# Mean squares by quarters of tokens in column tiles, PSUM banks kept whole in a planned four-layer graph network

## The chip, the cores and the metric

The kernel runs on one core of a Trainium2 chip. The metric is the device time of one execution in microseconds, lower is better. The time before is the median of three runs. TensorE is called PE in profile rows, its weight loads PEld, VectorE DVE, ScalarE ACT, GpSimd POOL, SyncE SP.

## The reference

There are 64 graphs of 256 nodes with 256 features, and each has a dense 256x256 matrix `adj` of edge weights. Four layers follow each other; each is `x = layernorm(x + f(x, adj))`, all in float32.

```python
# layer 0: sigmoid attention of 4 heads, scaled by degrees
att = sigmoid(q @ k.T / 8) * adj;  deg = att.sum(-1);  A = deg**-.5 * att * deg**-.5;  f = layernorm(A @ v)
# layer 1: softmax attention of 8 heads, masked where adj <= 0
f = softmax(where(adj > 0, q @ k.T / sqrt(32), NEG)) @ v @ Wo + bo
# layer 2: sum over neighbours, then a network of 1024 hidden features
h = (eps * x + adj @ x) @ W1 + b1
f = silu(h * rsqrt(mean(h**2, -1) + 1e-6) * rms_weight) @ W2 + b2
# layer 3: additive attention of one head, layernorm, gelu
f = gelu(layernorm(softmax(where(adj > 0, leaky(s1[:, None] + s2[None, :]), NEG)) @ Wh) * gamma + beta)
```

The change is in layer 2's `mean(h**2, -1)`, the mean over 1024 hidden features for each of the 256 nodes, and in the way in which the order of all instructions is planned.

## The kernel before, in words

A graph's nodes lie in two blocks of 128 partitions (`NB = 2`), its features likewise. `graph()` does not issue instructions. It records operations with `op(engine, cost, fn, writes, reads, ...)`; an `Op` holds a closure `fn` that will issue one or several instructions on one engine, a planned cost in ns, and what it writes and reads (`Value`s, some in parts, such as the two halves of a PSUM tile). All 64 graphs are recorded first.

`Plan.order()` then puts all operations of all graphs into one order. It steps through a model of the five engines, and takes at each step the operation that can start first; among equals, the one that is due first. "Due" comes from turns: every graph has four turns, one for each table of ScalarE (sigmoid, exp, silu, gelu), and layers of different graphs share rounds (`ROUND = 0, 2, 5, 7`: layer 1 of a graph runs two rounds after its layer 0, layer 2 five rounds after, layer 3 seven rounds after). An operation without predecessors (a load) is admitted once its due time lies at most `AHEAD` turns away. Buffers are slots of a kind: `SLOTS` has 42 of "s" (512 words in SBUF), 3 of "b" (2048 words, `hT`), 8 of "p" (the eight PSUM banks), and so on. An operation that takes a buffer has to wait for a free slot.

The model knows modes of TensorE. "full" is a matmul on the whole 128x128 array, "transpose" is a transpose, "rows" has 32 or 64 rows (scores L444 and L524), "columns" has 32 or 64 columns (degrees L462, products with values L484 and L560). `CHANGE` holds the planned costs of going from one mode to another, and `STAY` makes the planner reluctant to leave rows or columns.

`emit()` issues the closures in the planned order. From there every engine works through its own queue in that order; semaphores are set automatically where one instruction depends on another. That tracking goes by whole PSUM banks: a matmul into one half of a bank is ordered against a read of the other half. The plan before counts the halves as independent.

The lines that matter: in layer 2, L591 forms `aggT` (neighbour sums), L603 multiplies it with W1, each PSUM bank taking two blocks of 128 hidden features (i = 0, 1). ScalarE reads each half twice: L608 squares into `sq`, L610 scales into `hT`. L615 adds the squares of the four banks, L617 the two halves. L622 sums over the partitions on TensorE: for each block of 128 nodes, `sq` is the stationary operand and a column `mean_of` of 1/1024 is the moving one, so the mean of a node comes out on its partition. L625 adds the epsilon, L626 (GpSimd) takes the power -1/2, and L631 transposes the two columns, broadcast over 128 columns, into `pr`, a row for each node on all partitions. L635 multiplies `hT` by it, L637 applies silu, L645 multiplies with W2.

In layer 1, L524 makes the scores of four heads at a time (`hq` = 0 and 1), four PSUM banks each, from `qT1` and `kT1` (L510, L311). L407 masks them and finds the row minimum on VectorE, L412 takes exp, L545 transposes on VectorE, L547 and L549 reorder through DRAM, L560 multiplies with `v1`. L565 to L573 bring the reciprocal row sums `r` to the partitions; L567 is a small transpose on TensorE. In layer 0, L462 sums over partitions with a 128x32 operand of ones in four column tiles, and L466 transposes 32x32 blocks of the result on VectorE. L287 is the same kind of transpose on other tiles; L320 and L331 are shared helpers for projections; L275 is the helper for transposes on TensorE; L660 and L669 belong to layer 3.

Of the kernel before, what the change touches and what calls it, by code (L numbers as in the profile page):

```python
# [9 lines left out]
F32 = mybir.dt.float32  # L10
AF = mybir.ActivationFunctionType
OP = mybir.AluOpType

P = 128
# [5 lines left out]
PE_MM, PE_TR = 432, 109  # L20
# [7 lines left out]
DMA_KB, DMA_SEEN = 4, 1900  # L28

WORDS = {"s": 516, "d": 1024, "b": 2048, "c": 32, "p": 512, "h": 1024}  # L30
AHEAD = 14
STAY = 200
NEAR = 1, 1, 3

ROUND = 0, 2, 5, 7
TAIL = 0, 2, 3, 4
# [42 lines left out]
class Plan:  # L79
# [6 lines left out]
        self.ops, self.turns = [], {}  # L86
        self.graph = 0

    def op(self, engine, cost, fn, w=(), r=(), turn=None, mode="full", after=None, size=0):
        pair = lambda x: x if isinstance(x, tuple) else (x, None)  # L90
        w, r = [pair(x) for x in w], [pair(x) for x in r]
        op = Op(engine, cost, fn, w, r, self.graph, turn, mode, after, size)
        op.table = turn is not None and engine == "ACT"
        if op.table:
            self.turns[turn] = self.turns.get(turn, 0) + 1
        self.ops.append(op)

    def order(self):
        for i, op in enumerate(self.ops):
            op.index = i  # L100
        for op in reversed(self.ops):
            op.due = min((nxt.due for nxt in op.after), default=4 * (min(op.graph + ROUND[3], self.graphs - 1 + TAIL[3]) + 1))
            if op.turn is not None:
                op.due = min(op.due, op.turn)
        clock = {e: 0.0 for e in AFTER}
        self.free = {k: [(0.0, i) for i in range(n)] for k, n in SLOTS.items()}
        turns, left = sorted(self.turns), dict(self.turns)
        turn, loaded, mode, moved = 0, None, "full", 0.0
        ready = {op for op in self.ops if not op.waits}
        done = []  # L110
        self.busy = {e: 0.0 for e in AFTER}
        while ready:
            best = None
            for op in ready:
                if (op.due - AHEAD if op.first else op.turn or 0) > turns[turn]:
                    continue
                start = clock[op.engine]
                if op.engine == "PE" and mode in ("rows", "columns") and mode != op.mode:
                    start += STAY - 60 * (op.mode == "transpose")
                start = max(start, op.ready)  # L120
                need = {}
                for v in op.values:
                    if v.slot is None:
                        need[v.kind] = need.get(v.kind, 0) + 1
                for kind, n in need.items():
                    free = self.free[kind]
                    if len(free) < n:
                        break
                    start = max(start, sorted(free)[n - 1][0])
                else:  # L130
                    key = start, op.due, op.graph, op.index
                    if best is None or key < best[0]:
                        best = key, start, op
            if best is None:
                raise RuntimeError(f"the plan is stuck at {len(done)} of {len(self.ops)}")
            _, start, op = best
            op.start = start
            ready.discard(op)
            if op.table and op.turn != loaded:
                op.start, loaded = op.start + TABLE_LOAD, op.turn  # L140
            if op.engine == "PE":
                op.start = max(op.start, clock["PE"] + CHANGE.get((mode, op.mode), 0))
                mode = op.mode
            end = clock[op.engine] = op.start + op.cost
            op.landed = end + op.seen
            if op.engine == "SP":
                moved = max(moved, end) + op.size * DMA_KB
                op.landed = max(op.landed, moved + DMA_SEEN)
            self.busy[op.engine] += op.cost
            done.append(op)  # L150
            op.takes = [v for v in op.values if v.slot is None]
            for v in op.takes:
                self.free[v.kind].sort()
                v.slot = self.free[v.kind].pop(0)[1]
            for v in op.values:
                v.uses -= 1
                v.end = max(v.end, op.landed)
                if not v.uses:
# [12 lines left out]
        return sorted(done, key=lambda op: op.start)  # L171
# [78 lines left out]
def graph(plan, nc, c, t, out, b):  # L250

    op = plan.op
# [264 lines left out]
    for hq in range(H1 // 4):  # L517
        pss = [Value("p", "ps", 2) for _ in range(4)]

        def fn(hq=hq, pss=pss):  # L520
            for n in range(NB):
                for i in range(4):
                    s = slice(i * HD1, (i + 1) * HD1)
                    pe.matmul(two(pss[i])[:, n, :], two(qT1)[s, hq, n * P:(n + 1) * P], two(kT1)[s, hq, :],  # L524
                              start=True, stop=True)
        op("PE", 2 * PE_MM, fn, pss, [qT1, kT1], turn=turn(1, EXP), mode="rows")
        for pair in range(2):
            e = Value("d", "e", 4)
            for i in range(2):
                softmax(pss[2 * pair + i], negmask, HD1 ** -0.5, e,  # L530
                        lambda n, i=i, e=e: e.t[:, 256 * (2 * i + n):256 * (2 * i + n + 1)],
                        lambda n, i=i: 2 * i + n, r, lambda n, h=4 * hq + 2 * pair + i: 2 * h + n, turn(1, EXP))
            if b < NEAR[1]:
                eT = Value("d", "eT", 2)
                for i in range(2):
                    half = lambda v, i=i: v.t[:, 512 * i:512 * (i + 1)].rearrange("p (n c) -> p n c", n=2)
                    ps = Value("p", "ps", 2)
                    transpose(lambda ps=ps: two(ps), lambda e=e, half=half: half(e), ps, e)
                    op("ACT", 466, lambda ps=ps, eT=eT, half=half: act.copy(half(eT), two(ps)), [(eT, i)], [ps])
                eTs.append((eT, lambda i, m, eT=eT: eT.t.rearrange("p (h m c) -> p h m c", h=2, m=2)[:, i, m]))  # L540
                continue


            eb, far, eT = Value("d", "eb"), Value("h", "far"), Value("d", "eT", 4)
            op("DVE", 1155, lambda e=e, eb=eb: dve.transpose(eb.t.rearrange("p (b g i) -> p g b i", b=4, i=32),  # L545
                                                             e.t.rearrange("p (g b i) -> p g b i", b=4, i=32)), [eb], [e])
            op("SP", 420, lambda eb=eb, far=far: nc.sync.dma_start(far.t, eb.t), [far], [eb], after=3500, size=512)  # L547
            for q in range(4):
                op("SP", 420, lambda far=far, eT=eT, q=q: nc.sync.dma_start(  # L549
                    eT.t[32 * q:32 * q + 32].rearrange("j (a g) -> j a g", a=4),  # L550
                    far.t.rearrange("(a j) (b g) -> b j a g", a=4, b=4)[q]), [(eT, q)], [far], after=4000, size=128)
            eTs.append((eT, lambda i, m, eT=eT: eT.t.rearrange("p (a h n k i) -> p h k n a i", a=4, h=2, n=2, k=2)[:, i, m]))
# [65 lines left out]
    ps = Value("p", "ps")  # L618

    def fn(ps=ps, sq=sq):  # L620
        for n in range(NB):
            pe.matmul(ps.t[:, n:n + 1], sq.t[:, n * P:(n + 1) * P], c.mean_of, start=True, stop=True)  # L622
    op("PE", 363, fn, [ps], [sq])
    rs = Value("c", "rs")
    op("DVE", 50, lambda ps=ps: dve.tensor_scalar(rs.t[:, :NB], ps.t[:, :NB], 1e-6, None, op0=OP.add), [rs], [ps])  # L625
    op("POOL", 700, lambda: pool.tensor_tensor(rs.t[:, :NB], rs.t[:, :NB], c.mhalf[:, :NB], OP.pow), [rs], [rs])  # L626
    pr = Value("p", "pr")

# [62 lines left out]
def gnn_stack_kernel(ctx: ExitStack, tc: tile.TileContext, t: dict, out: bass.AP):  # L691
# [25 lines left out]
    make_identity(nc, ident)  # L717
    ones = const.tile([P, 32], F32, name="ones")
    nc.vector.memset(ones, 1.0)
    mean_of = const.tile([P, 1], F32, name="mean_of")  # L720
    nc.vector.memset(mean_of, 1.0 / HID)
    mhalf = const.tile([P, 8], F32, name="mhalf")
    nc.vector.memset(mhalf, -0.5)
# [50 lines left out]
```

## Time and profile before

| | |
|---|---|
| median of three runs | 2768.54 us (2766.03 to 2769.21) |
| profiled execution, its own time | 2761.13 us |
| its span, first to last instruction | 2759.3 us |
| mean granted TensorE clock | 0.996 |
| first matmul starts / last matmul starts | 6.1 us / 2742.4 us |
| L622, TensorE rows of 128x1 | 256 rows, 34.8 us busy |
| L625, DVE | 64 instructions, 147 ns each |
| L626, POOL | 64 instructions, 755 ns each |

Times below are counted from the start of the span. A row of the timeline has start, length, engine, line, operation, tiles, shape and the number of instructions merged in it; a float32 matmul is two instructions there, a transpose one. In the table of stretches, each row has the stretch, its length, busy time and (instruction count) of PE, PEld, DVE, ACT and POOL, then the granted clock, the share of the DMA engines and GB/s. A matmul's length overlaps with the next, so distances between starts are more exact than lengths.

### The profile page before, as it was taken

To read this page: it belongs to the slowest core of one execution; us is meant where nothing else is said; L and a number is where in the kernel's file an instruction comes from. 1 tells how busy PE (TensorE), PEld (TensorE's weight loads), DVE (VectorE), ACT (ScalarE), POOL (GpSimd) and SP (SyncE) were. 2 spreads that over 40 slices of the span, in tenths; PEclk is the share of its full clock that TensorE was granted. 3 is DMA by queue.
4 is the path that set the end of the run, shared out by engine and by line. 5 is a ranking of instruction groups with operands and counts; after the bars stand their busy time and mean duration, and the time that the engine had idled before them with its cause. 6 is when DMAs were issued, how large, how long until landed. Compare 5 with 4: busy or idle time off the path is not lost.

```text
span 2759.3 us, 56034 instructions
## 1 busy us (share of the span) xinstructions
PE 2703.5 (98%) x17280; PEld 2160.5 (78%) x17280; DVE 2443.0 (89%) x7426; ACT 2224.2 (81%) x5323; POOL 574.6 (21%) x902
## 2 busy tenths in 40 slices
PE   8999999999999999999999999999999999999997
PEld 6778777777777777787877877788778777777776
DVE  6989998898898889989989989889989899899966
ACT  4878888778788888788878887888888887888775
POOL 1112222122121121221221212212212122122212
PEclk9999999999999999999999999999999999999999
DMA  5677677676677566766756756757667677576651
GB/s 157 199 210 198 172 204 201 176 205 167 193 215 191 157 192 173 211 176 189 210 161 190 217 158 195 211 152 209 184 176 212 166 189 218 143 206 188 184 135 35
DMA packets 710923, 505.17 MB, mean 183 GB/s; under 512 B 310112, under 2 KB 669920, under 8 KB 710624
## 3 DMA queue, kind: packets, MB, share of 16 engines
q1 hardware_dynamic: 710624, 501.59, 65.9%
q8 instruction: 138, 2.26, 0.3%
q14 instruction: 161, 1.32, 0.2%
HBM read 303.44 MB, written 197.92 MB: 182 GB/s over the span
## 4 chain that ended last, share of the span: by engine, by line
PE 75%; DVE 10%; ACT 6%; DMA 4%; SPq 2%; issue 2%; POOL 0%; DVEq 0%; POOLq 0%; ACTq 0%
PE ps L331 13%; PE ps L320 13%; PE ps L645 13%; PE ps L603 11%; PE ps L444 4%; PE ps L524 4%; PE ps L484 3%; PE av L560 3%; PE ps L660 3%; PE ps L591 3%; ACT e L412 2%; DVE e L407 2%; DVE st L345 1%; DMA eT<-far 1%; PE ps L275 1%
## 5 line engine op out<-in xcount | busy, mean ns | idle before, releaser
L412 ACT ACTIVATE e<-e,low 128x256 f32<-128x256 f32 x1152 | 579.8, 505 | 87.5 <-DVE low L407 86.6
L645 PE MATMUL ps<-w,hT 128*128 128x256 f32 x2048 | 478.8, 383 | 5.5 <-ACT hT L637 4.8
L603 PE MATMUL ps<-aggT,w 128*128 128x256 f32 x2048 | 476.4, 382 | 3.8 <-DVE low L407 1.9
L357 POOL TENSOR_SCALAR mv<-mv 128x2 f32<-128x2 f32 x384 | 123.0, 320 | 1573.3 <-DVE mv L347 1012.1
L645 PEld LDWEIGHTS ps<-w,hT 128*128 128x128 f32 x2048 | 382.4, 191 | 68.1 <-issue 6.7
L603 PEld LDWEIGHTS ps<-aggT,w 128*128 128x128 f32 x2048 | 379.7, 190 | 69.4 <-DVE low L407 11.7
L407 DVE CUSTOM_DVE_ANT_0 e<-ps,adj 128x256 f32<-128x256 f32 x1024 | 361.1, 420 | 12.7 <-PE ps L524 11.2
L545 DVE STREAM_TRANSPOSE eb<-e 128x1024 f32<-128x1024 f32 x252 | 306.2, 1224 | 9.3 <-ACT e L412 9.2
L608 ACT ACTIVATE sq<-ps,b 128x256 f32<-128x256 f32 x512 | 242.0, 480 | 82.7 <-PE ps L603 73.0
L358 POOL TENSOR_TENSOR mv<-mv,mhalf 128x2 f32<-128x2 f32 x384 | 298.6, 778 | 32.0
L610 ACT ACTIVATE hT<-ps,br,r 128x256 f32<-128x256 f32 x512 | 288.8, 575 | 10.2 <-PE ps L645 6.7
L372 ACT ACTIVATE x<-y,mv 128x256 f32<-128x256 f32 x384 | 217.3, 602 | 50.9 <-DVE mv L368 48.9
L345 DVE BATCH_NORM_STATS2 st<-y 128x6 f32<-128x256 f32 x640 | 245.2, 413 | 0.9
L412 ACT ACTIVATION_READ_ACCUMULATOR e<-e,low 128x1 f32 x1152 | 225.4, 196 | 0.0
L615 DVE TENSOR_TENSOR sq<-sq 128x512 f32<-128x512 f32 x192 | 131.0, 682 | 98.1 <-ACT sq L608 97.2
L450 DVE TENSOR_TENSOR att<-att,adjT 128x512 f32<-128x512 f32 x256 | 166.6, 681 | 5.1 <-ACT att L448 5.1
L524 PE MATMUL ps<-kT,qT 32*128 32x256 f32 x2048 | 152.0, 400 | 4.3 <-ACT kT L311 4.2
L635 DVE TENSOR_TENSOR hT<-hT,pr 128x1024 f32<-128x1024 f32 x128 | 149.7, 1209 | 5.3 <-PE pr L631 5.3
L470 POOL TENSOR_TENSOR dp<-dp,mhalf 128x8 f32<-128x8 f32 x64 | 106.8, 1668 | 196.3 <-DVE dp L469 166.2
L448 ACT ACTIVATE att<-ps 128x512 f32<-128x512 f32 x256 | 132.2, 603 | 5.6 <-PE ps L444 3.0
L637 ACT ACTIVATE hT<-hT 128x1024 f32<-128x1024 f32 x128 | 128.9, 1050 | 9.1 <-DVE hT L635 7.9
L524 PEld LDWEIGHTS ps<-kT,qT 32*128 32x128 f32 x2048 | 97.9, 184 | 47.5 <-issue 23.3
(113 smaller groups left out, 5486.0 us busy)
## 6 DMA issues: line engine op xcount, KB each, us to landing
far<-eb SPq DMA_DIRECT2D x252, 512.0 KB, 3.8
eT<-far SPq DMA_DIRECT2D x1008, 128.0 KB, 3.9
adj<-in_adj SPq DMA_DIRECT2D x128, 256.0 KB, 4.6
far<-eb SPq DMA_DIRECT2D x488, 64.0 KB, 1.8
x0T<-in_xT SPq DMA_DIRECT2D x64, 256.0 KB, 3.6
adjT<-in_adjT SPq DMA_DIRECT2D x64, 256.0 KB, 4.4
x<-in_x SPq DMA_DIRECT2D x64, 256.0 KB, 4.8
adj<-in_adjT SPq DMA_DIRECT2D x64, 256.0 KB, 5.4
```

What stands on the lines that cost most here:

```text
L320: pe.matmul(two(ps)[:, o, :], w.t[:, k, o * P:(o + 1) * P], two(xT)[:, k, :], start=(k == 0), stop=(k == DB - 1))
L331: pe.matmul(two(ps)[:, n, :], two(xT)[:, k, n * P:(n + 1) * P], w()[:, k, :], start=(k == 0), stop=(k == DB - 1))
L345: op("DVE", 328, lambda n=n: dve.bn_stats(st.t[:, 6 * n:6 * n + 6], two(src)[:, n, :]), [(st, n)], [(src, n)])
L358: pool.tensor_tensor(m()[:, :, 2], m()[:, :, 2], c.mhalf[:, :NB], OP.pow)
L407: op("DVE", 345, lambda n=n: dve.tensor_tensor_reduce(out=E(n), in0=two(logits)[:, n, :], in1=two(negmask)[:, n, :], scale=-scale, scalar= ...
L412: op("ACT", 491, lambda n=n: act.activation(E(n), E(n), AF.Exp, bias=low.t[:, n:n + 1], scale=-1.0, accum_out=r.t[:, col(n):col(n) + 1]), ...
L524: pe.matmul(two(pss[i])[:, n, :], two(qT1)[s, hq, n * P:(n + 1) * P], two(kT1)[s, hq, :], start=True, stop=True)
L545: op("DVE", 1155, lambda e=e, eb=eb: dve.transpose(eb.t.rearrange("p (b g i) -> p g b i", b=4, i=32), e.t.rearrange("p (g b i) -> p g b i" ...
L603: pe.matmul(two(ps)[:, i, :], c.w2_1.t[:, k, (j + i) * P:(j + i + 1) * P], two(aggT)[:, k, :], start=(k == 0), stop=(k == DB - 1))
L608: op("ACT", 357, lambda ps=ps, sq=sq, i=i, j=j: act.activation(two(sq)[:, i, :], two(ps)[:, i, :], AF.Square, bias=c.b2_1.t[:, j + i:j + i ...
L610: op("ACT", 491, lambda ps=ps, i=i, j=j: act.activation(Hb(j + i)[:, 0], two(ps)[:, i, :], AF.Identity, bias=c.br2.t[:, j + i:j + i + 1], ...
L645: pe.matmul(two(ps)[:, n, :], Hb(j)[:, 0, n * P:(n + 1) * P], c.w2_2.t[:, j, :], start=(j == 0), stop=(j == HB - 1))
```

## The change

Four things change together.

1. In `Plan.op`, a dependency on part of a PSUM tile becomes one on the whole tile, for the plan alone.
2. The mean of squares is taken in column tiles. `mean_of` becomes 128x32 and stationary, `sq` is the moving operand, in four quarters: quarter g holds the nodes 32g to 32g+31 of both blocks, 64 columns, and writes partitions 32g to 32g+31. VectorE transposes the 128x64 result in 32x32 blocks into the unused second half of `sq`, and the epsilon instruction reads one column out of each block. The plan's mode for this operation is "columns".
3. Operations with the same `joint` key are joined: `join()` makes them one operation in the plan, whose closures are issued one right after the other. The first scores of layer 1 (`hq == 0`) of a graph b are joined with the means of graph b-3, where b+2 lies from 10 to 55 (46 graphs). The joined operation waits for the inputs of both and takes the buffers of both, five PSUM banks.
4. `AHEAD` goes from 14 to 12.

```diff
-AHEAD = 14
+AHEAD = 12
+JOINT = 10, 56
...
-        pair = lambda x: x if isinstance(x, tuple) else (x, None)
+        pair = lambda x: (x[0], None if x[0].kind == "p" else x[1]) if isinstance(x, tuple) else (x, None)
...
-        op.table = turn is not None and engine == "ACT"
+        op.table, op.joint, op.leaves = turn is not None and engine == "ACT", joint, mode
...
+    def join(self):
+        joints, before = {}, {}
...
+        for ops in joints.values():
+            if len(ops) == 1:
+                continue
+            ops.sort(key=lambda op: op.joint[1])
+            one, fns = ops[0], [op.fn for op in ops]
...
+            one.fn = lambda fns=fns: [fn() for fn in fns]
+            one.cost = sum(op.cost for op in ops) + sum(CHANGE[a.mode, b.mode] for a, b in zip(ops, ops[1:]))
+            one.leaves = ops[-1].mode
...
     def order(self):
         for i, op in enumerate(self.ops):
             op.index = i
+        self.join()
...
-                mode = op.mode
+                mode = op.leaves
...
-        op("PE", 2 * PE_MM, fn, pss, [qT1, kT1], turn=turn(1, EXP), mode="rows")
+        op("PE", 2 * PE_MM, fn, pss, [qT1, kT1], turn=turn(1, EXP), mode="rows", joint=((("a", b + 2), 0) if JOINT[0] <= b + 2 < JOINT[1] else None) if hq == 0 else None)
...
-        for n in range(NB):
-            pe.matmul(ps.t[:, n:n + 1], sq.t[:, n * P:(n + 1) * P], c.mean_of, start=True, stop=True)
-    op("PE", 363, fn, [ps], [sq])
+        for g in range(4):
+            pe.matmul(ps.t[g * 32:(g + 1) * 32, :64], c.mean_of,
+                      sq.t[:, :N].rearrange("p (m g t) -> p m g t", g=4, t=32)[:, :, g], start=True, stop=True)
+    op("PE", 109, fn, [ps], [sq], mode="columns", joint=(("a", b + 5), 1) if JOINT[0] <= b + 5 < JOINT[1] else None)
     rs = Value("c", "rs")
-    op("DVE", 50, lambda ps=ps: dve.tensor_scalar(rs.t[:, :NB], ps.t[:, :NB], 1e-6, None, op0=OP.add), [rs], [ps])
+    pm = lambda sq=sq: sq.t[:, N:N + 64]
+    op("DVE", 125, lambda ps=ps: dve.transpose(pm(), ps.t[:, :64]), [(sq, 1)], [ps])
+    op("DVE", 50, lambda: dve.tensor_scalar(
+        rs.t[:, :NB], pm().rearrange("p (n k) -> p n k", k=32)[:, :, 0], 1e-6, None, op0=OP.add), [rs], [(sq, 1)])
...
-    mean_of = const.tile([P, 1], F32, name="mean_of")
+    mean_of = const.tile([P, 32], F32, name="mean_of")
```

More of the change, by code (lines that the diff above doesn't have):

```diff
@@ L87, in __init__, with op @@
         self.graph = 0
-    def op(self, engine, cost, fn, w=(), r=(), turn=None, mode="full", after=None, size=0):
-        pair = lambda x: x if isinstance(x, tuple) else (x, None)
+    def op(self, engine, cost, fn, w=(), r=(), turn=None, mode="full", after=None, size=0, joint=None):
+        pair = lambda x: (x[0], None if x[0].kind == "p" else x[1]) if isinstance(x, tuple) else (x, None)
         w, r = [pair(x) for x in w], [pair(x) for x in r]
         op = Op(engine, cost, fn, w, r, self.graph, turn, mode, after, size)
-        op.table = turn is not None and engine == "ACT"
+        op.table, op.joint, op.leaves = turn is not None and engine == "ACT", joint, mode
         if op.table:
@@ L96, in op @@
         self.ops.append(op)
+    def join(self):
+        joints, before = {}, {}
+        for op in self.ops:
+            if op.joint is not None:
+                joints.setdefault(op.joint[0], []).append(op)
+            for nxt in op.after:
+                before.setdefault(nxt, []).append(op)
+        gone = set()
+        for ops in joints.values():
[3 more added lines that the diff above has]
+            one, fns = ops[0], [op.fn for op in ops]
+            prior = list(dict.fromkeys(p for op in ops for p in before.get(op, ())))
+            assert not set(prior) & set(ops)
+            for p in prior:
+                p.after = list(dict.fromkeys(one if nxt in ops else nxt for nxt in p.after))
+            one.after = list(dict.fromkeys(nxt for op in ops for nxt in op.after))
+            for nxt in one.after:
+                before[nxt] = list(dict.fromkeys(one if p in ops else p for p in before[nxt]))
+                nxt.waits = len(before[nxt])
+            before[one], one.waits = prior, len(prior)
+            one.fn = lambda fns=fns: [fn() for fn in fns]
+            one.cost = sum(op.cost for op in ops) + sum(CHANGE[a.mode, b.mode] for a, b in zip(ops, ops[1:]))
+            one.leaves = ops[-1].mode
+            one.turn = max((op.turn for op in ops if op.turn is not None), default=None)
+            values = [v for op in ops for v in op.values]
+            one.values = list(dict.fromkeys(values))
+            for v in one.values:
+                v.uses -= values.count(v) - 1
+            gone.update(ops[1:])
+        waits, ops, at = {op: op.waits for op in self.ops}, [op for op in self.ops if not op.waits and op not in gone], 0
+        while at < len(ops):
+            for nxt in ops[at].after:
+                waits[nxt] -= 1
+                if not waits[nxt]:
+                    ops.append(nxt)
+            at += 1
+        assert len(ops) == len(self.ops) - len(gone)
+        self.ops = ops
     def order(self):
```

## The prediction

> **What bounds the kernel now.** I read the page's busy table first, then the table of stretches, then the matmul rows of the timeline.
>
> ```profile
> PE 2703.5 (98%) x17280; PEld 2160.5 (78%) x17280; DVE 2443.0 (89%) x7426; ACT 2224.2 (81%) x5323; POOL 574.6 (21%) x902
> ...
> PE 75%; DVE 10%; ACT 6%; DMA 4%; SPq 2%; issue 2%; POOL 0%; DVEq 0%; POOLq 0%; ACTq 0%
> ```
>
> Here the reader sees that the matmul engine is never free for long, and that three quarters of the chain that ended last is its own work. VectorE is second with 11% idle.
>
> ```profile
> 300.00:1000.00 700.00, 692.45 (x4415) 555.12 (x4411) 637.92 (x1944) 574.80 (x1372) 149.61 (x237) 1.00 0.69 192
> 1000.00:1700.00 700.00, 695.87 (x4474) 554.93 (x4467) 629.81 (x1914) 577.91 (x1386) 147.49 (x230) 1.00 0.67 185
> 1700.00:2600.00 900.00, 893.54 (x5743) 713.81 (x5742) 816.84 (x2489) 737.64 (x1761) 195.49 (x304) 1.00 0.68 187
> 2600.00:2700.00 100.00, 93.54 (x528) 76.14 (x529) 73.09 (x215) 76.70 (x184) 15.29 (x28) 0.97 0.56 144
> ```
>
> From 300 to 2600 us the second column leaves TensorE only 18 us idle in 2300. So the time is what the matmul stream costs, plus some 40 us of ramp, drain and early waits. Busy hides what a piece of the stream really costs, so I price by distances between starts:
>
> ```profile
> 1338.16 1.89 PE L603 MATMUL ps<-aggT,w 128*128 128x256 f32 x8
> 1339.98 1.15 PE L524 MATMUL ps<-kT,qT 32*128 32x256 f32 x16
> 1341.06 0.28 PE L567 MATMUL ps<-ident,r 128*16 128x128 f32 x1
> 1341.17 1.03 PE L603 MATMUL ps<-aggT,w 128*128 128x256 f32 x4
> 1342.13 1.95 PE L484 MATMUL ps<-att,v 128*64 128x256 f32 x16
> 1344.01 1.93 PE L560 MATMUL av<-eT,v 128*32 128x256 f32 x32
> 1345.76 0.62 PE L462 MATMUL ps<-added,ones 128*32 128x128 f32 x16
> 1346.31 1.15 PE L524 MATMUL ps<-kT,qT 32*128 32x256 f32 x16
> 1347.38 0.61 PE L622 MATMUL ps<-mean_of,sq 128*128 128x1 f32 x4
> 1347.85 1.97 PE L331 MATMUL ps<-v,eT 128*128 128x256 f32 x8
> 1349.66 0.59 PE L331 MATMUL ps<-w_o,yT 128*128 128x256 f32 x2
> ```
>
> Each matmul shows as two rows (a transpose as one). Over the whole trace a full 128x256 row has a median step of 216 ns. Eight are 1.728 us, yet L603 at 1338.16 is followed after 1.82: **going into a tiled form costs 93 ns**. L524 takes 1.075 us to the next start, and L484 1.88. A full run just after a tiled one is 100 ns longer (none when L567 stands between). L622 takes 0.47 us after tiled work, 0.364 after full work, and the full run after it is 81 ns longer (1347.85 to 1349.66 is 1.81).
>
> **What the Trainium skill says.** "TensorEngine Tiling (Array Packing)", Key Properties, says a change of tiling mode drains the engine; the trace agrees (93 ns in). The same page, Instruction Overhead, says that a matmul of one column takes as long as one of 60; in the trace L622 is far from free, 364 ns for two matmuls of one column. "TensorE: Matmul & The Clock Gate", LDWEIGHTS, prices a load by its columns, divided by 1.2 in ns: 27 ns for 32. The trace disagrees: 128x32 f32 took 106 to 110 ns (L462), so I use that. "PSUM — Partial Sum Buffer", Terms, says that TensorE and a reading engine on one bank and quadrant at once is an error; the waits agree only in that TensorE does wait for readers of a bank's other half, as below.
>
> **The change, part by part.** Instruction counts are from the built order of both programs, prices from the trace.
>
> *Mean squares removed.* L622 stands 64 times: 51 x 0.364 + 13 x 0.468 = 24.6 us, and 58 full runs behind it pay 81 ns = 4.7. Together 29.3 us, all on TensorE.
>
> *Mean squares added.* Four 128x32 weight loads with 64 columns each, eight rows. No row of this size exists; the nearest is L462 (128 columns). There the second pass starts 134 ns after the first because its loads need 107, the four starts are 7 apart, and the next form starts 201 after the last, of which about 107 is streaming and 94 leaving. With half the columns: 134 + 20 + 53 + 94 = 0.30 us. Bounds: 0.227 if the second pass need not wait for its loads (60 instead of 134), 0.355 if the last start holds as long as L462's. I take 0.30, as the loads do not shrink: 64 x 0.30 = 19.2 us (14.5 to 22.7).
>
> *What the tie and the new order do to mode changes.* 46 graphs' means stand right behind a first group of layer 1 scores, so they bring no entry of their own. But the whole order is replanned. Entries into tiled forms go from 279 to 277 (-0.2 us); full runs straight behind tiled work from 167 to 191 (+2.4); transposes there (55 ns each) from 38 to 25 (-0.7); the two score groups of a graph run together twice instead of ten times (2 x 1.075 instead of 1.995, +1.2); and column forms next to each other, which save 114 ns behind L560 and 24 in front, lose 2.1 us. Sum +4.8.
>
> TensorE's stream: -29.3 + 19.2 + 4.8 = **-5.3 us** (-10.0 to -1.8).
>
> *Whole banks in the plan.* In the order before, 21 matmul groups (17 of L603, 4 of L331) write half a bank after ACT or DVE was put to read the other half. Their gaps above the usual step add up to 2.5 us, 1.8 of it in one place (449.9 us, L603 waiting for L610). In the new order no such group is left. I take **-2**, between -2.5 and +2: a reader now waits for both halves, 0.86 us later, and ACT has 19% idle to take that.
>
> *VectorE.* 64 transposes of 128x64 out of PSUM are added. L466 (256 columns) has a mean of 432 ns and L287 (512) of 697, so 1.035 ns a column and 167 fixed: 0.233 us, 14.9 in all; busy goes from 88.5% to about 89.3%. The added epsilon (L625, 147 ns) only changes where it reads. VectorE does not set the end, but softmax (L407), which frees score banks, queues behind it. Also POOL's power and the two transposes L631 now come 0.23 us plus a semaphore later. TensorE loads waited for POOL there 22 times (8.2 us), matmuls only 7 times (1.6 us). Between 0 and 22 x 0.33 = 7 us; I take **+1**, as L631 is placed by the plan, which counts the transpose.
>
> *Loads admitted 12 turns ahead instead of 14.* Four turns are one graph, 2759/64 = 43 us, so 129 us remain before use against a landing of 3.6 to 5.4 us. Nothing; that margin hides it. The SP queue keeps its 3598 DMAs; ACT's instructions do not change, nor do POOL's.
>
> Sum: -5.3 - 2 + 1 = **-6.3 us**. The profiled execution took 2761.1 (span 2759.3 and 1.8 around it), so it would go to 2754.8. The median of the runs is 7.4 above the profiled one; the same difference taken from 2768.5 gives 2762.
>
> **The rivals.**
>
> *Slower: the tied pair waits.* The pair needs five free banks out of eight at once, qT1 and kT1 of one graph, and the summed squares of the graph three places before; the later of the two orders holds TensorE, and everything queued behind waits. For it: L622 already waited for VectorE (DVE sq 1.7 us, five times, in the matmul waits), L524 for kT (4.2 us, seven times). Against: these are a few times in 64, and the plan can place the pair where both are ready. At 0.14 us for each of 46 pairs the gain is gone; at 0.4 us it is 18 us, so 2781; with half of them waiting so, about 2771.
>
> *No change: the waits move.* TensorE's stream shrinks by 5 us, but a VectorE with 15 us more work releases banks later. For it: TensorE's gaps that name L407. Against: VectorE has 316 us idle. With waits up by 5: 2767.
>
> *A larger gain.* About 50 us of gaps longer than usual are left in the stream, 13 of them in the last 160 us. A plan whose banks are right might shed a fifth: 2752. The same term could go up as easily, since every piece moves.
>
> *The column form is no cheaper.* If leaving and loading bring the new piece to 0.38 us, the stream gains nothing and only the banks count: 2767.
>
> **How the numbers follow.** About 0.2% (5.5 us) is what a measurement of this kernel can tell. Chances: forecast and its neighbourhood 0.38, larger gain 0.27, no change 0.10, column form no cheaper 0.05, tied pair waits 0.20. Faster by over 0.2%, below 2763: the lower two thirds of the first (0.25) and all of the second, 0.52. Slower: the tied pair, and 0.02 for an unlucky order in the others, 0.22. Within: the rest, 0.26. The range takes the stream's lower bound with some 9 us of shed waits downwards, and the half-waiting pair with 7 us of other waits upwards: 2749 to 2778.
>
> **What would show it.** In the profile after: no 128x1 rows; 512 rows of 128*32 with 64 columns, and about 0.30 us from their first start to the next form's; 64 new VectorE transposes near 0.23 us; POOL and ACT counts as before; TensorE idle between 300 and 2600 us near 18 us. If the new piece takes under 0.25 us the stream gains more than I said. If TensorE's waits at layer 1's scores or at the new means exceed 12 us in sum, the tied pair is the cause and I am wrong. If the gain comes mostly from the first 300 or last 160 us, the sum was right only by chance.

## The result, and the profile after

| | before | after |
|---|---|---|
| median of four runs each | 2767.62 us (2766.03 to 2769.21) | 2724.91 us (2721.57 to 2725.96) |
| span of the profiled execution | 2759.3 us | 2719.8 us |
| mean granted TensorE clock | 0.996 | 0.994 |
| first matmul starts | 6.1 us | 6.7 us |
| last matmul's start to the end of the span | 16.9 us | 14.3 us |

The ratio is 0.9847 [0.9831, 0.9862]: the change makes the kernel 42.7 us faster. The prediction had the direction, and said 6. The two profiled executions lie 39.5 us of span apart; the sums below are of these.

The page of the kernel after, busy table and chain that ended last:

```profile
PE 2677.9 (98%) x17536; PEld 2140.4 (79%) x17536; DVE 2447.8 (90%) x7490; ACT 2226.1 (82%) x5323; POOL 570.5 (21%) x902
...
PE 89%; DMA 3%; DVE 3%; ACT 2%; SPq 2%; issue 1%; POOLq 0%; DVEq 0%; ACTq 0%; POOL 0%
```

TensorE's share is 98% as before, so the busy table doesn't show the difference. The chain does: TensorE's own work makes up 89% of it where it was 75%, and VectorE 3% where it was 10%. The table of stretches of the kernel after:

```profile
300.00:1000.00 700.00, 693.18 (x4586) 553.59 (x4584) 645.99 (x1975) 584.75 (x1398) 152.94 (x236) 1.00 0.70 193
1000.00:1700.00 700.00, 700.00 (x4590) 563.04 (x4590) 647.31 (x1976) 590.01 (x1406) 149.62 (x237) 1.00 0.69 192
1700.00:2600.00 900.00, 894.16 (x5897) 715.19 (x5894) 831.84 (x2571) 746.42 (x1795) 190.61 (x305) 1.00 0.68 190
2600.00:2720.00 120.00, 100.33 (x537) 82.08 (x535) 78.94 (x234) 80.93 (x182) 22.38 (x44) 0.92 0.30 77
```

From 1000 to 1700 us TensorE is never idle. Read the number of instructions beside the busy time: 4590 where it was 4474, in the same 700 us, although TensorE was busy for 695.87 of them before. Of the 116 more, some 68 are the four rows that each new mean has more (about 17 graphs in 700 us); the rest shows that the matmuls before lay further apart while they counted as busy. The row of 700 to 2300 us, before and then after:

```profile
700.00:2300.00 1600.00, 1586.56 (x10162) 1267.74 (x10161) 1442.01 (x4395) 1313.93 (x3144) 337.85 (x530) 1.00 0.68 188
```
```profile
700.00:2300.00 1600.00, 1599.36 (x10592) 1282.54 (x10591) 1475.87 (x4525) 1344.09 (x3211) 340.83 (x540) 1.00 0.68 190
```

TensorE gains 13 us of busy time in these 1600, and 4% of instructions (of these 4%, 1.5% are the four more of each new mean, 256 in the whole kernel). In the timeline after, a tied pair:

```profile
1328.11 0.28 PE L613 MATMUL ps<-ident,r 128*16 128x128 f32 x1
1328.32 1.15 PE L570 MATMUL ps<-kT,qT 32*128 32x256 f32 x16
1329.39 0.32 PE L668 MATMUL ps<-sq,mean_of 128*32 128x64 f32 x8
1329.64 1.99 PE L377 MATMUL ps<-v,eT 128*128 128x256 f32 x8
1331.57 1.15 PE L570 MATMUL ps<-kT,qT 32*128 32x256 f32 x16
```

L570 are layer 1's scores (L524 before), L668 the new means: 0.25 us from their start to the next form's.

**Stream and waits.** To separate what TensorE's work costs from what it waits for, I priced the whole order of matmuls of each kernel with the median distance between starts for each pair of forms in the traces, as in the prediction. The sum is called the stream; what the time from the first matmul's start to the last's has above it is called waits. So everything that makes a step longer than usual counts as waits, a slower TensorE too.

| us | before | after | change | predicted |
|---|---|---|---|---|
| stream | 2667.6 | 2657.7 | -9.9 | -5.3 |
| waits | 68.8 | 41.1 | -27.7 | -1 |
| ahead of the first matmul and behind the last | 23.0 | 21.0 | -2.0 | 0 |
| sum, against 39.5 of span | | | -39.6 | -6.3 |

Step by step along the trace, late steps alone add up so: up to 700 us 19 to 20 us in both kernels; from 700 to 2300 us 38 before, about 1 after; behind 2300 us about 21 and 19. Before, this makes 79, more than the 68.8 of the table, since steps that follow a late one are often shorter than usual and make some of it good. With those set against them, the middle has some 29 us before and 1 after, which is the whole change of the waits. **The gain is waits that were spread thinly over the middle**, just under 2 us in every 100. The longest waits in 700 to 2300 us between VectorE and ScalarE show what was thin (waiter, releaser, us in total, times, longest). Before:

```profile
DVE sq L615 <- ACT sq L608: 65.6, 50, 4.6
...
ACT e L412 <- DVE low L407: 61.6, 41, 4.8
```

After:

```profile
ACT sq L654 <- PE ps L649: 49.5, 78, 1.7
...
ACT e L458 <- DVE low L453: 46.3, 53, 1.3
...
DVE sq L661 <- ACT sq L654: 22.6, 13, 2.6
```

Before, VectorE stood up to 4.6 us for ScalarE's squares, and ScalarE up to 4.8 us for VectorE's softmax minimum. Over all lines, ScalarE waited 128 us for VectorE and VectorE 102 us for ScalarE in these 1600 us; after, 53 and 25. Both now wait more for TensorE instead, ScalarE 178 us where it was 134. How waits of these two engines turn into TensorE's is not shown here: they say where the order ran tight, not what each late matmul waited for.

### The profile page after: what moved, and what is told of

It is laid out like the page before. It is cut to its first block, busy times and chain, and to the rows that moved or that the text cites. A ratio compares the mean times of both kernels' runs of the same rounds, so it can differ in the third digit from the quotient of the medians.

```text
span 2719.8 us, 56662 instructions
## 1 busy us (share of the span) xinstructions
PE 2677.9 (98%) x17536; PEld 2140.4 (79%) x17536; DVE 2447.8 (90%) x7490; ACT 2226.1 (82%) x5323; POOL 570.5 (21%) x902
## 4 chain that ended last, share of the span: by engine, by line
PE 89%; DMA 3%; DVE 3%; ACT 2%; SPq 2%; issue 1%; POOLq 0%; DVEq 0%; ACTq 0%; POOL 0%
PE ps L695 16%; PE ps L366 15%; PE ps L377 15%; PE ps L649 14%; PE ps L570 4%; PE ps L490 4%; PE ps L530 4%; PE av L606 4%; PE ps L637 4%; PE ps L710 4%; PE ps L321 1%; PE ps L508 1%; ACT e L458 1%; DMA far<-eb 1%; DVE e L453 1%
## 5 line engine op out<-in xcount | busy, mean ns | idle before, releaser
L458 ACT ACTIVATE e<-e,low 128x256 f32<-128x256 f32 x1152 | 573.8, 500 | 60.4 <-DVE low L453 59.2
L403 POOL TENSOR_SCALAR mv<-mv 128x2 f32<-128x2 f32 x384 | 131.6, 343 | 1586.2 <-DVE mv L393 1126.2
L649 PE MATMUL ps<-aggT,w 128*128 128x256 f32 x2048 | 459.0, 380 | 0.6 <-ACT att L494 0.6
L649 PEld LDWEIGHTS ps<-aggT,w 128*128 128x128 f32 x2048 | 386.0, 190 | 56.0 <-issue 1.5
L654 ACT ACTIVATE sq<-ps,b 128x256 f32<-128x256 f32 x512 | 226.2, 473 | 83.3 <-PE ps L649 64.9
L404 POOL TENSOR_TENSOR mv<-mv,mhalf 128x2 f32<-128x2 f32 x384 | 286.8, 747 | 32.1
L656 ACT ACTIVATE hT<-ps,br,r 128x256 f32<-128x256 f32 x512 | 266.1, 576 | 29.4 <-PE ps L695 29.3
L458 ACT ACTIVATION_READ_ACCUMULATOR e<-e,low 128x1 f32 x1152 | 219.5, 191 | 0.0
L570 PE MATMUL ps<-kT,qT 32*128 32x256 f32 x2048 | 146.5, 400 | 0.0
L377 PE MATMUL ps<-v,eT 128*128 128x256 f32 x512 | 130.8, 393 | 7.1 <-ACT hT L656 3.5
```

The lines of the kernel that those rows point to most:

```text
L377: pe.matmul(two(ps)[:, n, :], two(xT)[:, k, n * P:(n + 1) * P], w()[:, k, :], start=(k == 0), stop=(k == DB - 1))
L404: pool.tensor_tensor(m()[:, :, 2], m()[:, :, 2], c.mhalf[:, :NB], OP.pow)
L458: op("ACT", 491, lambda n=n: act.activation(E(n), E(n), AF.Exp, bias=low.t[:, n:n + 1], scale=-1.0, accum_out=r.t[:, col(n):col(n) + 1]), ...
L649: pe.matmul(two(ps)[:, i, :], c.w2_1.t[:, k, (j + i) * P:(j + i + 1) * P], two(aggT)[:, k, :], start=(k == 0), stop=(k == DB - 1))
L654: op("ACT", 357, lambda ps=ps, sq=sq, i=i, j=j: act.activation(two(sq)[:, i, :], two(ps)[:, i, :], AF.Square, bias=c.b2_1.t[:, j + i:j + i ...
L656: op("ACT", 491, lambda ps=ps, i=i, j=j: act.activation(Hb(j + i)[:, 0], two(ps)[:, i, :], AF.Identity, bias=c.br2.t[:, j + i:j + i + 1], ...
```

## The experiments

"Repeats every n" below says that the order of operations on TensorE between one graph's layer 0 scores and the next's is, in the middle of the program, the same again n graphs later. One correction to some expectations: they say that the kernel before, or the one with the bank rule alone, doesn't repeat. Compared over longer distances, both repeat every 14 graphs, though only over about half of the middle. The ratios are to runs of the kernel before in the same session, whose medians lie between 2765.0 and 2768.0.

| kernel | median us | ratio to before [95%] | stream | waits | repeats every |
|---|---|---|---|---|---|
| before | 2767.6 | 1 | 2667.6 | 68.8 | 14 |
| after | 2724.9 | 0.9847 [0.9831, 0.9862] | 2657.7 | 41.1 | 3 |
| no_bank_rule | 2736.5 | 0.9876 [0.986, 0.9892] | 2657.5 | 53.9 | 3 |
| no_tie | 2780.6 | 1.0039 [1.0028, 1.005] | 2664.1 | 95.8 | not |
| ahead_14 | 2729.7 | 0.9853 [0.9838, 0.9868] | 2658.5 | 45.5 | 1 |
| old_mean_tied | 2801.8 | 1.0114 [1.0096, 1.0132] | 2671.7 | 107.8 | 2 |
| only_bank_rule | 2758.3 | 0.997 [0.9963, 0.9977] | 2671.5 | 64.8 | 14 |
| only_columns | 2804.1 | 1.0128 [1.0099, 1.0157] | 2659.1 | 120.8 | not |
| only_tie | 2772.2 | 1.0023 [1.0016, 1.0031] | 2670.7 | 74.3 | 1 |
| tie_and_columns | 2750.8 | 0.9942 [0.9921, 0.9963] | 2657.2 | 69.6 | in part |
| busier_dve_before | 2822.7 | 1.0201 [1.0181, 1.0221] | 2667.6 | 127.9 | 14 |
| busier_dve_after | 2758.7 | 0.9966 [0.9956, 0.9977] | 2657.7 | 77.5 | 3 |
| ahead_13 | 2767.5 | 1.0001 [0.9991, 1.0011] | 2658.1 | 90.3 | not |
| tie_6_60 | 2723.7 | 0.9848 [0.9834, 0.9863] | 2651.3 | 52.0 | 2 |
| late250_before | 2758.5 | 0.9968 [0.9955, 0.9981] | 2678.1 | 54.1 | 9 |
| late250_no_tie | 2791.7 | 1.0096 [1.0071, 1.012] | 2667.3 | 96.1 | not |
| late250_ahead_13 | 2736.2 | 0.9881 [0.9866, 0.9896] | 2647.8 | 61.2 | 1 |
| late250_after | 2725.1 | 0.9843 [0.9828, 0.9858] | 2657.3 | 44.4 | 1 |

### One edit undone

**no_bank_rule**: the plan's dependencies on halves of banks again.

```diff
-        pair = lambda x: (x[0], None if x[0].kind == "p" else x[1]) if isinstance(x, tuple) else (x, None)
+        pair = lambda x: x if isinstance(x, tuple) else (x, None)
```

> The changed kernel with the first edit undone: the plan again counts the halves of a PSUM bank as independent. TensorE's stream priced from the order is the same as after the change (2657.5 against 2657.7 us), so only waits can move. Theory 'repeating order': the tie makes the plan repeat every three graphs (its order still does so here), and a repeating order has nothing that comes late; then 2725 within 8 us. Theory 'true banks': the plan before put reads and writes on one bank that the chip orders anyway, and the waits come from there; then most of the 24 to 29 us of waits come back, 2745 to 2755.

It is 11.6 us slower than after, 3.5 more than the theory 'repeating order' allowed. Its middle is as free of waits as after's (1.4 us of late steps in 700 to 2300); the loss lies in the first 700 us, 32 us of late steps for 19. The bank rule isn't what empties the middle.

**no_tie**: no operation is joined, the other three edits stay.

```diff
-JOINT = 10, 56
+JOINT = 0, 0
```

> The changed kernel without the tie (no pair is joined); banks, column means and 12 turns stay. Its order does not repeat. The stream priced from the order is 6.5 us dearer (330 entries into tiled forms instead of 277). 'Repeating order' expects those 6.5 plus most of the waits of the kernel before: 2750 to 2765. 'True banks' expects the 6.5 alone and a little: 2730 to 2736.

The whole gain is gone and 13 us more (2780.6), though the stream is still 3.5 us cheaper than before. The waits are 95.8 us, more than either theory expected. The same two waits of its middle between VectorE and ScalarE:

```profile
DVE sq L661 <- ACT sq L654: 39.7, 27, 5.8
ACT e L458 <- DVE low L453: 32.4, 19, 6.3
```

The long ones are back, up to 6.3 us each. In sum the two lines are no more than in after (72 and 69 us), so it is not their total that tells the kernels apart.

**ahead_14**: `AHEAD` as before.

```diff
-AHEAD = 12
+AHEAD = 14
```

> The changed kernel with loads admitted 14 turns ahead again. The order still repeats (every graph), the stream is priced 0.9 us dearer. Both theories expect 2724 to 2732; a third, 'later loads leave buffers free', expects waits to come back: 2740 or more.

4.8 us slower than after, and still repeating, now every graph.

**old_mean_tied**: the means of before (two matmuls of one column, no transpose on VectorE), still joined to the scores.

```diff
-    op("PE", 109, fn, [ps], [sq], mode="columns", joint=(("a", b + 5), 1) if JOINT[0] <= b + 5 < JOINT[1] else None)
+    op("PE", 363, fn, [ps], [sq], joint=(("a", b + 5), 1) if JOINT[0] <= b + 5 < JOINT[1] else None)
```

> The changed kernel with the old mean (two matmuls of one column, on the full array), still tied behind layer 1's first scores, banks and 12 turns as after. The order repeats every two graphs; the stream is priced 14 us dearer. 'Repeating order' expects those 14 us and no waits in the middle: 2738 to 2745. If the column form has a share beyond its stream price (VectorE or the later chain), the difference is not 14.

2801.8 us, slower than before, although the stream costs only 4 us more; 2738 to 2745 was expected. Its row of 700 to 2300 us, and the longest waits of matmuls in the whole run:

```profile
700.00:2300.00 1600.00, 1543.11 (x9850) 1228.60 (x9849) 1402.30 (x4258) 1269.90 (x3052) 335.69 (x512) 1.00 0.65 181
```
```profile
PE ps L691 <- DVE mv L393: 27.2, 19, 1.6
PE ps L321 <- ACT x L418: 12.9, 19, 0.7
PE ps L715 <- ACT att L494: 10.5, 15, 0.9
```

TensorE is idle for 57 us of these 1600. The order repeats every two graphs, and the same waits come in every period: 19 times the same one of 1.4 us. **Repeating alone is not enough**; what repeats can be a wait. Here the plan itself had it: by its own times TensorE stands idle for 32 us between 700 and 2300 us, where the orders of before and after have 2 and 1.

### One or two edits alone, added to the kernel before

```diff
 only_bank_rule
-        pair = lambda x: x if isinstance(x, tuple) else (x, None)
+        pair = lambda x: (x[0], None if x[0].kind == "p" else x[1]) if isinstance(x, tuple) else (x, None)
 only_columns (with the transpose on VectorE and the wider mean_of)
-    op("PE", 363, fn, [ps], [sq])
+    op("PE", 109, fn, [ps], [sq], mode="columns")
 only_tie (with join(), the means as before)
-    op("PE", 363, fn, [ps], [sq])
+    op("PE", 363, fn, [ps], [sq], joint=(("a", b + 5), 1) if JOINT[0] <= b + 5 < JOINT[1] else None)
 tie_and_columns: the two together
```

> The kernel before with the bank rule in the plan alone (old mean, no tie, 14 turns). Stream priced from the order: 2671.5 us, 4 more than before; the order does not repeat. If the rule by itself takes waits away, 2750 to 2760; if only a tied order does, waits stay at 70 to 100 us as in the two untied orders seen so far: 2768 to 2800.

> The kernel before with the column means alone (VectorE transpose included; no tie, no bank rule, 14 turns). Stream priced from the order 2659.1 us, 8.4 less than before. If the column form is worth its stream price and the untied order's waits stay near 69: 2759. If untied orders scatter by tens of us, anything from 2750 to 2785.

> The kernel before with the tie alone (old mean tied behind layer 1's first scores; halves of banks independent, 14 turns). The order repeats every graph in the middle; stream priced 3 us more than before. If repeating is enough, 2735 to 2745. If a repeating order only repeats what its one period holds, as the old mean with all other edits did (108 us of waits), 2770 to 2800.

> The kernel before with the tie and the column means (no bank rule, 14 turns). If those two edits make the gain, 2725 to 2740. If bank rule and 12 turns are needed to make the repeating period free of waits, 2750 or more.

The bank rule alone lowers the median by 0.3%; its profiled execution doesn't show where (waits -4.0, stream +3.9, span 2759.1 for 2759.3). The columns alone make the stream 8.5 us cheaper and the kernel 36 us slower, 19 us beyond the widest range expected: 120.8 us of waits, the most of all orders without the added work below. The tie alone is slightly slower as a whole, but between 900 and 2100 us it has no waits at all; some 45 us of its 74 lie behind 2300 us. The tie and the columns together save 17 us, the bank rule and `AHEAD` in addition 26 more. `AHEAD` alone was not run. The effects don't add up: 0.997, 1.0128 and 1.0023 alone, 0.9847 with `AHEAD` together. An edit has no fixed price here; most of its effect is that of the order that it makes.

### Does a busier VectorE explain the waits?

The rival theory: waits depend on how much slack VectorE has at each point, whatever the order. In both kernels the addition in `plus_row` is issued twice at an unchanged planned cost, so the planned order is the same as of before or of after, and VectorE has 192 more instructions of 678 ns, 130 us in all. The second addition writes the same sums again.

```diff
-        op("DVE", 602, lambda: dve.tensor_tensor(two(xb), two(x), row_b(r.t), OP.add), [xb], [x, r])
+        op("DVE", 602, lambda: [dve.tensor_tensor(two(xb), two(x), row_b(r.t), OP.add) for _ in range(2)], [xb], [x, r])
```

> The changed kernel with every sum of x and a bias row on VectorE made twice (192 more instructions of 678 ns, 130 us, VectorE near 95% busy); the plan does not know, so the order is the same. Theory 'slack': in the repeating order VectorE and ScalarE run as far ahead as buffers let them, so a busier VectorE is absorbed in the middle: 5 to 20 us longer. If no slack is there: 40 us or more.

> The kernel before with the same 192 instructions more on VectorE and the same order as before. 'Slack' expects the order that doesn't repeat to take it worse than the changed kernel: 30 to 80 us longer. If both kernels grow by about the same, the slack of the repeating order is not what saved its waits.

The rows of 700 to 2300 us, before and then after, each with the doubled addition:

```profile
700.00:2300.00 1600.00, 1568.04 (x9896) 1248.43 (x9895) 1478.67 (x4397) 1283.31 (x3071) 332.16 (x518) 0.99 0.67 183
```
```profile
700.00:2300.00 1600.00, 1592.14 (x10418) 1274.60 (x10418) 1532.97 (x4591) 1333.78 (x3165) 348.04 (x536) 1.00 0.68 190
```

The order of before loses 55 us and that of after 34, which lies between the two cases of its expectation. In the middle, from the layer 0 scores of graph 15 to those of graph 50, after loses 0.56 us a graph (41.17 to 41.73) and before 0.86 (42.31 to 43.17). By late steps alone, after gets 28 us in 700 to 2300 us, where it had about 1. So slack matters, and the order of after has more of it. But these 28 us, with VectorE busy for 96% of the stretch, are fewer than the 38, counted likewise, of the kernel before, with VectorE busy for 90%: a busy VectorE is not by itself what costs them.

### Is it the repeating order?

**ahead_13** has all four edits, the tie included, with `AHEAD` 13: TensorE's work and all other engines' are the same as in after, but the order doesn't repeat.

```diff
-AHEAD = 12
+AHEAD = 13
```

> All four edits, but loads admitted 13 turns ahead: the pair is still tied in 46 graphs, yet the order does not repeat anywhere. Stream priced from the order 2658.1 us, 0.4 more than after. If tying the pair by itself saves the waits: 2722 to 2735. If it is the repeating order that saves them: waits of 65 to 100 us as in the orders that don't repeat, 2748 to 2785.

2767.5 us: the whole gain is gone, with a stream of 2658.1 (after 2657.7). Its chain, its row of 700 to 2300 us and one of its waits there:

```profile
PE 74%; DVE 10%; DMA 7%; SPq 4%; ACT 3%; issue 2%; POOL 0%; DVEq 0%; POOLq 0%; ACTq 0%
```
```profile
700.00:2300.00 1600.00, 1579.32 (x10344) 1262.46 (x10343) 1455.45 (x4446) 1318.83 (x3162) 345.32 (x531) 0.99 0.69 189
```
```profile
ACT e L458 <- DVE low L453: 66.4, 35, 6.2
```

The chain is that of the kernel before (74%, 10%), and ScalarE's waits for the softmax minimum have a mean of 1.9 us and reach 6.2, where after has 0.9 and 1.3. This run decides most: no theory that goes by the amount of work, by the tie's direct effect or by the banks can tell ahead_13 from after. It shows that the order alone is worth the whole gain. That the repeating is what matters in the order, and not another trait of it, rests on the comparison of all kernels below.

Not all that is called waits here is waiting. In ahead_13 TensorE has three gaps between 1399 and 1408 us (3.1, 1.4 and 2.2 us idle). What follows the last one, and the stretches around it:

```profile
1407.42 3.68 PE L366 MATMUL ps<-xT,w_q 128*128 128x256 f32 x8 [2.19 <-ACT xT L357]
1410.93 1.89 PE L366 MATMUL ps<-xT,w_k 128*128 128x256 f32 x8
1412.66 1.89 PE L637 MATMUL ps<-adj,x 128*128 128x256 f32 x8
```
```profile
1400.00:1410.00 10.00, 3.67 (x22) 2.52 (x23) 9.09 (x22) 8.14 (x19) 2.49 (x3) 0.70 0.40 72
1410.00:1420.00 10.00, 10.00 (x75) 7.33 (x78) 5.13 (x23) 5.90 (x20) 1.85 (x2) 0.96 0.32 65
```

Eight full rows take 3.51 us to the next start, and the eight behind them 1.73; the granted clock is 0.70 in the first 10 us and 0.96 in the next. An estimate from such doubled steps in stretches of half the granted clock gives 6 us of the 35 (net) that ahead_13 has between 700 and 2300 us, 8 in no_tie and in only_columns. The kernels before and after have none there, so this has no part in the gain; but orders with longer gaps pay for them twice.

**tie_6_60**: the tie for 54 graphs instead of 46.

```diff
-JOINT = 10, 56
+JOINT = 6, 60
```

> The changed kernel with the pair tied for b+2 from 6 to 59 (54 graphs). The order repeats every two graphs over a longer middle; stream priced from the order 2651.3 us, 6.3 less than after, since entries into tiled forms fall to 245. If the repeating middle is free of waits again: 2705 to 2722, faster than after. If its period holds waits of its own, as the old mean tied did: 2740 or more.

The same time as after (2723.7), just outside the range of the better case, made up differently: a stream 6.4 us cheaper, and waits 10.9 us higher, some 0.5 to 2 us in every 100 of the middle, spread evenly, as if its period of two graphs had some built in.

### Are the waits those of a plan whose handovers are too short?

`AFTER` holds the plan's time from the end of an operation to the start of what depends on it, for each engine. If real handovers between VectorE and ScalarE take longer than planned, a longer planned handover should empty the middle of any order.

```diff
-AFTER = {"PE": 230, "DVE": 150, "ACT": 190, "POOL": 180, "SP": 3000}
+AFTER = {"PE": 230, "DVE": 400, "ACT": 440, "POOL": 180, "SP": 3000}
```

> The kernel before, its plan counting 250 ns more from the end of a VectorE or ScalarE instruction to the start of what needs it. The order does not repeat; the stream priced from it is 2678.1 us, 10.6 more than before. If handovers planned too short make the waits of such orders: waits of 30 to 45 us, 2730 to 2748. If only repetition removes them: 65 us or more, 2765 to 2800.

> The changed kernel without the tie, with the same 250 ns. The order does not repeat; stream 2667.3 us, waits without the 250 ns were 96 us. 'Handovers': 2720 to 2740. 'Repetition': 2755 to 2790.

> All four edits with 13 turns and the 250 ns. Now the order repeats every graph, and the stream is priced 2647.8 us. Without the 250 ns it did not repeat and had 90 us of waits. Both theories expect few waits: 2700 to 2720, faster than the changed kernel.

> The changed kernel with the 250 ns; repeats every graph, stream 2657.3 us as after. Both theories: 2715 to 2730. If waits exceed 55 us, a repeating order is no guarantee.

late250_no_tie still doesn't repeat and keeps its waits (96.1 us, 95.8 without the longer handover): the theory isn't supported. late250_ahead_13 now repeats every graph, its middle has no waits (61.2 us in all lie at the ends, 17.7 of them between 2500 and 2600 us), and it takes 2736.2 us where ahead_13 took 2767.5, yet 16 us more than the most that was expected. late250_before repeats every 9 graphs instead of 14 and has 54.1 us of waits for 68.8, with a stream that is 10.5 us dearer; its time lies between the two ranges expected, and since its period changed as well, it tells nothing apart. late250_after is like after.

**Over all eighteen kernels**: the four whose order doesn't repeat have 90 to 121 us of waits; those with periods of 9 and 14 graphs, unburdened, 54 to 69; those with periods of one to three, unburdened, have 41 to 74, and nearly none in the stretch that repeats; the exceptions are old_mean_tied (107.8) and, mildly, tie_6_60, whose periods contain waits. tie_and_columns, which repeats in part, has 69.6. No version beats after by an amount that can be measured.

What stays open is why a plan that doesn't repeat leaves such waits on the chip. The plan's own times hardly hold them: between 700 and 2300 us these leave TensorE idle, mode changes counted as work, for 2.3 us in before, 1.3 in after, 1.8 in ahead_13, 3.4 in no_tie, 7.1 in only_columns and 18.6 in late250_no_tie. The whole planned spans of before and after are 2703.4 and 2697.4 us, 6 us apart, as forecast; those of ahead_13 and ahead_14 are 2704.1 and 2703.8, where 38 us were measured between them. Handovers planned too short by a fixed time were not it for no_tie.

## Why the prediction was wrong

**The failed step is the term for the waits of the replanned order.** I wrote that some 50 us of gaps were left, that the plan might shed a fifth, and that "the same term could go up as easily, since every piece moves"; the forecast then set it to -1 (banks -2, VectorE +1). It measured -27.7, and from kernel to kernel it runs from 41 to 121 us with practically the same work. So it was the largest term, and the only one that I didn't work out. The 50 us were themselves too few: by the same steps, summed over the whole kernel, before has 68.8. The repeating could have been seen blind: the built order of both programs was at hand, and after's repeats every three graphs. The forecast direction came true in part by luck: the stream explains 10 of the 42.7 us, and the same four edits with `AHEAD` 13 gain nothing.

**The bound was misread.** "18 us idle in 2300" came from the busy column, which counts a matmul that starts late behind a modelled end as busy (a full row is drawn some 380 ns long where the next starts after 216). In 700 to 2300 us of before it shows 13 us idle; the steps between starts show some 29 us of waits, or 38 by late steps alone. I had the steps for single pieces and didn't sum them over the stretch. "TensorE idle from 300 to 2600 us near 18" became 12.7 us, a small change in the wrong view.

**The new means.** Predicted 0.30 us, measured 0.249 (median): within the bounds, near the lower. The second pass started 80 ns after the first (60 after the last of its four starts), where I had 134, so it did not wait for the ends of its four loads, which take 109 ns each as expected. The rest of the piece came as predicted: 149 ns from the last start to the next form for 147. With 64 x 0.051 that is 3.3 us of the 4.6 by which the stream fell further than I said; the other 1.3 I did not separate. The clause "under 0.25 us" thus came true by a hair, and with it the rival of a column form that is no cheaper (0.38 us) is false.

**Mode changes and means removed.** The rows of 128x1 are gone, 512 rows of 128x64 are there, and the sum holds apart from the above.

**Whole banks.** -2 for the waits seen at half-written banks. Undoing the rule costs 11.6 us, nearly all in the first 700 us, adding it alone brings 0.3%. It acts through the order, which my count of 21 groups could not show.

**VectorE.** The transpose, from the groups of the kernel after:

```profile
L673 DVE STREAM_TRANSPOSE sq<-ps x64: 222/245/251, 126.6 to 2667.5; 128x64 f32<-128x64 f32 x64
```

Median 245 ns, predicted 233. The waits of matmuls over the whole run of after:

```profile
PE ps L366 <- DMA x0T<-in_xT: 6.7, 1, 6.7
PE ps L695 <- ACT hT L687: 4.0, 1, 4.0
PE ps L668 <- DVE sq L663: 0.6, 2, 0.3
```

No matmul waits for the transpose, and the means wait twice for the summed squares, 0.6 us: **the rival of the waiting tied pair is false**. The gain didn't come from the ends either, and the rival of waits that only move, with 5 us more of them, is false.

**AHEAD at "nothing".** Wrong. The margin of the loads is as large as I said, but the number also enters the choice of what comes next: 12 to 13 costs 42.6 us, 12 to 14 costs 4.8.

**The rival of a larger gain** had the right term, waits shed by the new order. It was mis-sized, and put down to the banks, which alone bring 0.3%: 40% of the waits went, not a fifth, and with the cheaper stream that ends 27 us below its 2752.

## What to carry to other kernels

Where a planner orders everything anew, compare the built orders before pricing the edits: in this kernel an order that repeats after a few graphs had hardly any waits in its middle (unless the repeated piece held one), and one that doesn't had 90 us or more in all, for nearly the same instructions. That is what eighteen orders of one kernel have in common, not a rule with a known cause, and the planner's own times did not tell ahead_13 from ahead_14. Measure waits of a bound engine by the distances between starts against the usual ones, early ones set against late ones, summed over a stretch, since its busy share hides thin ones. Where the order can turn over with one constant, try several values of it, and give a forecast a range that spans the waits of all orders.

## What the runs showed of the hardware

- In a piece of two passes over four column tiles, 128x32 f32 operands of 109 ns load time each and 64 columns of movement, the second pass started 80 ns after the first (60 after the last of its four starts); with 128 columns (L508) it takes 133 (113). I had expected the loads to hold both.
- The next form starts 149 ns after the last start of such a piece, and only 36 ns if it is another piece of four column tiles (ten cases in after: the degrees, L508, and products with values, L606).
- In ahead_13, eight full 128x256 rows behind gaps of TensorE took 3.51 us to the next start, the next eight 1.73 (427 and 216 ns a row), with a granted clock of 0.70 in the 10 us around the first and 0.96 in the next 10.
- 130 us more of work for VectorE, which had 272 us idle in after and 316 in before, cost 34 and 55 us: the idle time of an engine that is not the bound took up most of the added work, but not all of it.
